# Which half of PSUM comes first: turning the pairs round behind two rounds, and when slots and squares are handed out

## The chip, the cores and the metric

The kernel runs on one core of one Trainium2 chip. The metric is the device time in microseconds of one execution; the median of three runs is taken. The profile and the trace are of one further execution on the same core.

## What is computed

The input `x` is a batch of 8 elements of 8 channels of 512 x 512 numbers in float32. Two layers follow each other.

Layer 0 normalizes each element by groups of channels, keeps a few low Fourier modes of every second row and column, mixes the channels in them with complex weights, transforms back and adds the result to `x`. Layer 1 normalizes again and computes three things from the result:

```python
for _ in range(STEPS):                      # 15 steps
    mapped = R * grid * (1.0 - grid)
    local = _conv(mapped, K_local, groups=C_OUT)          # 3x3, each channel by itself
    physics = (1.0 - EPS) * mapped + EPS * local
    grid = (1.0 - BETA) * physics + BETA * drive
cml_out = jnp.clip(grid, 0.0001, 1.0 - 0.0001)
h = jax.nn.relu(_conv(x, Wp, bp))                         # 3x3, 8 to 128 channels
nca_out = jax.nn.sigmoid(_conv(h, Wu, bu))                # 1x1, 128 to 8
gin = jnp.concatenate([x, cml_out, nca_out], axis=1)
g = jax.nn.sigmoid(_conv(jax.nn.relu(_conv(gin, Wg1, bg1)), Wg2, bg2))
return g * cml_out + (1.0 - g) * nca_out
```

## The kernel before

The program is written out without loops on the chip. Each engine gets its instructions in the order in which the Python source issues them, and waits by semaphores where data or a buffer is not ready. The source issues the work in ticks. An element takes 75 ticks (`TICKS`), called t = 0 to 74 here. One call of `work` is one tick, and in it stand, in this order:

- **Two sets of the 15-step loop.** A half element is 4 channels, cut into 5 sets. A set is a tile `m` of 128 partitions by 4 x 514: 4 slabs (or channels) of 32 rows, with 3 rows of overlap. It holds a squared form of the grid, so one step is a 3x3 convolution by 48 matmuls on 32 x 32 parts of the array (L536, 96 instructions in the profile), an addition of the drive by VectorE in two halves (L591), and a square by ScalarE (L597). The first set writes the pairs `pairs[:2]` of PSUM, the second `pairs[2:]`. PSUM is held as 4 pairs of two banks, so that is all of it.
- **None to two rounds** of the convolution from 8 to 128 channels (`Hidden.round`, L636), the first in `pairs[:2]`, the second in `pairs[2:]`. The relu of the first pair of each is ScalarE's (L642), that of the second pair VectorE's (L644). Both write one tile `h`.
- **Squares** (`Half.squares`, `Half.square`): before step 1 of a set, ScalarE makes its `m` from the drive `dE` (L516), and GpSimd fills the two border columns (L515). This is done in the tick before the set's first step.
- **Other work**, in this order: `others.first` (a gate convolution L706, or one or two pieces of the next element's layer 0, such as L338, L433, L401, L305, L313), then, after every second round, `hidden.point` (L655: 8 matmuls on the two `h` tiles of the last two rounds, the first round's four first; the result is copied into or added to `y`, L662 or L664, and after four rounds the sigmoid L668 follows), then `others.second` (a gate's point L723, or another piece of layer 0).
- **tick()**, which runs what was put off: `later(1, work)` runs work at the end of the next tick. The stores of finished sets (L577, in `leave`), of `y` (L671) and of layer 0's result, and the exchange of overlap rows (L566) come this way.

Of the four pairs, `work` gives the letters `a` (first piece or gate convolution), `b` (a second piece in front of the point), `c` (the point) and `d` (the gate's point, or a piece behind the point):

```python
a, b, c, d = (pairs[i] for i in ((0, 1, 3, 2), (2, 0, 3, 2))[rounds == 1])
```

SBUF tiles of the 15-step loop live in 15 slots (`Slots`), taken from the left of a queue of free names and put back at its right. Per half, 10 drives (`dE` and `dO` for each of 5 sets, four DMAs of 256 KB each, L494) and 5 tiles `m` need one. `Half.fetch` loads drives in each tick as long as slots are free; all of these DMAs, like nearly all others, are issued on SP's queue, in order. A drive is dropped in `settle` at one of the last two steps, an `m` in `store`, right behind the issue of its four stores. Squares of the first half fall in t = 74, 0 and 1, those of the second half in t = 36, 37 and 38.

After the last element's sets, 40 ticks of two rounds and six of none finish the rounds and gates that are left.

Of the kernel before, what the change touches and what calls it, by code (L numbers as in the profile page):

```python
# [128 lines left out]
def conv_layers(ctx: ExitStack, tc: tile.TileContext, a, out):  # L129
# [27 lines left out]
    sets, shared = Slots("set", 15), Slots("shared", SHARED)  # L157
# [7 lines left out]
    pairs = [pp.tile([P, 2, N], F32, name=f"pair{i}") for i in range(4)]  # L165
# [4 lines left out]
    def later(ticks, work):  # L170
        put_off.append((now[0] + ticks, work))

    def tick(end=False):
        now[0] += 1
        due = [w for at, w in put_off if end or at <= now[0]]
        put_off[:] = [] if end else [(at, w) for at, w in put_off if at > now[0]]
        for work in due:
            work()
# [296 lines left out]
    class Half:  # L475
# [27 lines left out]

        def squares(self, n):
            for k in range(SETS):
                if k - 2 in (n, n + 1):
                    self.square(k)

        def fetch(self, n):
# [21 lines left out]
    def convolve(m, c0, step, ps):  # L531
        for n, dx in enumerate((1, 0, 2)):
            for t in range(4):
                for h in range(4):
                    at = slice(32 * h, 32 * h + 32)
                    nc.tensor.matmul(  # L536
                        ps[h // 2][32 * t : 32 * t + 32, h % 2],
                        band[at, c0 + (t if step % 2 else h), dx],
                        m[at, t, dx : dx + N],
                        start=(n == 0), stop=(n == 2), tile_position=(32 * h, 32 * t),  # L540
                    )
# [26 lines left out]
    def leave(m, k, half):  # L568

        g = m[:, :, 1 : N + 1]  # L570
        nc.vector.tensor_scalar(g, g, 0.0001, 1.0 - 0.0001, ALU.max, ALU.min)  # L571

        def store():
            for h in range(4):
                s = 4 * k + h
                lo, hi = SHARES[s]
                nc.sync.dma_start(  # L577
                    out=half.cml[1 + STARTS[s] + lo : 1 + STARTS[s] + hi, half.c0 : half.c0 + 4],
                    in_=g[32 * h + lo : 32 * h + hi],
                )  # L580
            sets.drop(m)

        later(1, store)

    def settle(half, step, k, ps):

        m, d = half.m[k], half.d[k, step % 2]
        u = m[:, :, 1 : N + 1]
        for q in range(2):
            at = slice(2 * q, 2 * q + 2)  # L590
            nc.vector.scalar_tensor_tensor(  # L591
                u[:, at], ps[q], FLOOR, d[:, at], ALU.max, ALU.add
            )
            if q:
                yield
            if step < STEPS:
                nc.scalar.square(u[:, at], u[:, at])  # L597
        if step == 1:
            half.drive(k, 0)
        elif step == STEPS - 2:  # L600
            nc.gpsimd.tensor_scalar(d, d, 0.5, None, ALU.add)  # L601
        elif step >= STEPS - 1:
            sets.drop(d)
        if step == STEPS:
            leave(m, k, half)
        elif (step - k) % HALO == 0:
            later(1, lambda: renew(half.m, k, step))
# [284 lines left out]
    def work(sets, rounds, e, after, transfers, squares=lambda: None):  # L892

        settled = iter(())
        for (half, step, k), ps in zip(sets, (pairs[:2], pairs[2:])):
            convolve(half.m[k], half.c0, step - 1, ps)
            next(settled, None)
            settled = settle(half, step, k, ps)
            next(settled)
            others.finish()  # L900
        others.finish()
        transfers()
        for ps in (pairs[:2], pairs[2:])[:rounds]:
            e.hidden.round(ps, after, settled)
        next(settled, None)
        squares()

        a, b, c, d = (pairs[i] for i in ((0, 1, 3, 2), (2, 0, 3, 2))[rounds == 1])

        point = rounds and e.hidden.n % 2 == 0  # L910
        others.first([a, b if point else c])
        if point:
            e.hidden.point(c[:, 0])
        others.second([d if point else c])
        tick()

    elements = [e]
    for n in range(-FIRST_ROUNDS, 0, 2):
# [2 lines left out]
    for b in range(B):  # L921
# [5 lines left out]
        done, rounds = e.hidden.n, ROUNDS if after else ROUNDS_LAST  # L927
        for t in range(TICKS):
            assert not after or t < TICKS - 5 or not after.pieces
            halves = [(e.first, 2 * t), (e.second, 2 * t - TICKS)]  # L930
            if after:
                halves.append((after.first, 2 * t - 2 * TICKS))
            for half, n in halves:
                half.prepare(n)

            def squares():
                for half, n in halves:
                    half.squares(n)

            def transfers():  # L940
                others.feed(t)
                for half, n in halves:
                    half.fetch(n)

            now_sets = []
            for n in (2 * t, 2 * t + 1):
                half = (e.first, e.second)[n // TICKS]
                now_sets.append((half, n % TICKS // SETS + 1, n % SETS))

            more = done + (t + 1) * (rounds - done) // TICKS - e.hidden.n  # L950
            work(now_sets, min(more, 2 - e.hidden.n % 2), e, after and after.hidden, transfers, squares)
# [66 lines left out]
```

## Time and profile before

| what | value |
|---|---|
| median of three runs (lowest to highest) | 9907.52 us (9905.83 to 9934.52) |
| the profiled execution | 9903.73 us, its span 9901.9 us |
| TensorE busy | 9355.4 us, 94% |
| VectorE, ScalarE, GpSimd busy | 5876.2 (59%), 4301.9 (43%), 1762.5 us (18%) |
| granted TensorE clock, mean over the span | 0.988 |
| convolution of a set, L536 | 4093.8 us busy in 115200 instructions |
| rounds, L636 | 2862.1 us in 24576 |
| point, L655 | 995.0 us in 8192, 136.2 us idle before |
| squares, L516 | 80 of 1.99 us each |
| relus, L642 and L644 | 1024 each, 1.12 and 1.28 us each |
| moved in HBM | 992.42 MB read, 268.78 MB written, mean 127 GB/s |

A group's row gives the line of the source, the engine, the operation, output and inputs, the shapes and the count; behind the bar come the busy time and the mean of one in ns, then the engine's idle time just before these instructions and what ended most of it. In a row of waits stand who waited, for whom, and the total, the number and the longest. In the timeline stand the start and the duration in us, and in brackets the idle time before.

### The profile page before, as it was taken

Reading aid. Unit: us, or ns where it says so; the run is one execution under the profiler, and the core shown is the slowest. Engines: PE = TensorE matmul, PEld = TensorE weight load, DVE = VectorE, ACT = ScalarE, POOL = GpSimd, SP = SyncE. Lnnn points to the kernel's source line nnn. Section 1 sums busy time; section 2 is a strip of 40 time slices with the busy share of each in tenths; the row PEclk is TensorE's granted clock in tenths of the full one; section 3 lists DMA queues with packets and bytes.
Section 4 is the critical chain, followed back from the end, with each engine's and each line's share of the span. In section 5 each row is a group of like instructions: output and inputs, shape, how many; then the busy total and the mean of one; then the engine's idle time right before and its main releaser. Section 6 shows DMA issues by size and latency. Waiting matters only on the chain. (4 is left out here: it accounts for less than half of the span.)

```text
span 9901.9 us, 353033 instructions
## 1 busy us (share of the span) xinstructions
PE 9355.4 (94%) x160496; PEld 4299.0 (43%) x160496; DVE 5876.2 (59%) x6067; ACT 4301.9 (43%) x4445; POOL 1762.5 (18%) x1406
## 2 busy tenths in 40 slices
PE   6999999999999999999999999999999999898999
PEld 3444444444444434444344444444434444444433
DVE  5665555665566655666556655566555665555655
ACT  2544444443444434444444444445444454344423
POOL 2010111103121131111312013120221202221212
PEclk9999999999999999999999999999999999999999
DMA  5241355446544465445655356652665525753688
GB/s 152 86 121 34 80 141 135 138 126 167 139 129 142 129 162 138 133 128 136 163 140 143 117 141 162 145 157 94 148 164 139 161 97 142 171 124 95 147 200 202
DMA packets 625130, 1353.61 MB, mean 137 GB/s; under 512 B 72570, under 2 KB 72698, under 8 KB 593618
## 3 DMA queue, kind: packets, MB, share of 16 engines
q1 hardware_dynamic: 621280, 1329.89, 51.3%
q8 instruction: 1261, 20.66, 0.9%
q14 instruction: 235, 1.93, 0.1%
q10 hardware_dynamic: 2354, 1.14, 0.0%
HBM read 992.42 MB, written 268.78 MB: 127 GB/s over the span
## 5 line engine op out<-in xcount | busy, mean ns | idle before, releaser
L536 PE MATMUL pair<-m,band 32*32 32x512 f32 x115200 | 4093.8, 605 | 212.5 <-issue 99.6
L597 ACT ACTIVATE m<-m 128x1024 f32<-128x1024 f32 x2240 | 2363.7, 1055 | 2812.8 <-DVE m L591 2685.0
L536 PEld LDWEIGHTS pair<-m,band 32*32 32x32 f32 x115200 | 2258.3, 103 | 1955.8 <-issue 983.1
L636 PE MATMUL pair<-cols,w_p 32*128 32x511 f32 (+1 forms) x24576 | 2862.1, 603 | 47.0 <-issue 15.9
L591 DVE SCALAR_TENSOR_TENSOR m<-pair,dO 128x1024 f32<-128x1024 f32 x1280 | 1506.5, 1219 | 1384.6 <-PE pair L536 1214.6
L636 PEld LDWEIGHTS pair<-cols,w_p 32*128 32x128 f32 x24576 | 1275.9, 186 | 1645.0 <-issue 1116.1
L591 DVE SCALAR_TENSOR_TENSOR m<-pair,dE 128x1024 f32<-128x1024 f32 x1120 | 1318.8, 1219 | 1075.4 <-PE pair L536 870.9
L644 DVE TENSOR_SCALAR h<-pair,b_p 128x1024 f32<-128x1024 f32 x1024 | 1313.0, 1283 | 812.1 <-PE pair L636 803.3
L642 ACT ACTIVATE h<-pair,b_p 128x1024 f32<-128x1024 f32 x1024 | 1141.4, 1115 | 1044.1 <-PE pair L636 1043.9
L655 PE MATMUL pair<-h,w_u 128*32 128x512 f32 x8192 | 995.0, 598 | 136.2 <-DVE h L644 124.7
L729 POOL TENSOR_TENSOR mix<-mix 96x512 f32<-96x512 f32 x344 | 438.0, 1273 | 3809.0 <-ACT mix L727 3598.7
L706 PE MATMUL pair<-gin,w_g 128*32 128x511 f32 (+1 forms) x8256 | 965.9, 601 | 31.1 <-DMA gin<-nca 17.0
L711 POOL TENSOR_TENSOR mix<-mix 96x512 f32<-96x512 f32 x344 | 446.9, 1299 | 2006.1 <-DMA mix<-nca 1276.1
L601 POOL TENSOR_SCALAR dO<-dO 128x2048 f32<-128x2048 f32 x80 | 431.9, 5411 | 1228.5 <-DVE m L591 1228.5
L655 PEld LDWEIGHTS pair<-h,w_u 128*32 128x32 f32 x8192 | 249.0, 110 | 756.7 <-issue 384.7
L706 PEld LDWEIGHTS pair<-gin,w_g 128*32 128x32 f32 x8256 | 235.8, 110 | 711.3 <-issue 471.6
L668 ACT ACTIVATE y<-y,b_u 128x512 f32<-128x512 f32 x256 | 184.7, 721 | 808.5 <-DVE y L664 808.3
L734 DVE SCALAR_TENSOR_TENSOR mix<-mix,back 96x512 f32<-96x512 f32 x344 | 327.0, 951 | 147.3 <-POOL mix L729 147.3
L662 ACT COPY y<-pair 128x512 f32<-128x512 f32 x256 | 149.8, 585 | 599.8 <-PE pair L655 490.3
L716 DVE TENSOR_SCALAR mix<-pair,b_g 128x512 f32<-128x512 f32 x344 | 257.9, 750 | 247.8 <-PE pair L706 247.8
L723 PE MATMUL pair<-mix,w_g 128*32 128x512 f32 x2064 | 356.5, 593 | 10.5 <-DVE mix L716 8.5
L529 POOL TENSOR_SCALAR dO<-dO,base 128x512 f32<-128x512 f32 x320 | 238.6, 763 | 437.1 <-DMA dO<-xn 246.3
(86 smaller groups left out, 2661.4 us busy)
## 6 DMA issues: line engine op xcount, KB each, us to landing
gin<-xn SPq DMA_DIRECT2D x344, 384.0 KB
cols<-xn SPq DMA_DIRECT2D x256, 512.0 KB
x<-in_x SPq DMA_DIRECT2D x120, 1024.0 KB
gin<-cml SPq DMA_DIRECT2D x344, 320.0 KB
gin<-nca SPq DMA_DIRECT2D x344, 320.0 KB
dE<-xn SPq DMA_DIRECT2D x320, 256.0 KB
dO<-xn SPq DMA_DIRECT2D x320, 256.0 KB
mix<-xn SPq DMA_DIRECT2D x344, 192.0 KB
```

The lines of the kernel that those rows point to most:

```text
L536: nc.tensor.matmul(ps[h // 2][32 * t : 32 * t + 32, h % 2], band[at, c0 + (t if step % 2 else h), dx], m[at, t, dx : dx + N], start=(n == ...
L591: nc.vector.scalar_tensor_tensor(u[:, at], ps[q], FLOOR, d[:, at], ALU.max, ALU.add)
L597: nc.scalar.square(u[:, at], u[:, at])
L601: nc.gpsimd.tensor_scalar(d, d, 0.5, None, ALU.add)
L636: nc.tensor.matmul(ps[g // 2][:, g % 2, lo:hi], w_p[p, dx, i % 2], self.cols[p, i // 2, at : at + hi - lo], start=(n == 0), stop=(n == 2), ...
L642: nc.scalar.activation(h[:, :2], ps[0], AF.Relu, bias=b_p)
L644: nc.vector.tensor_scalar(h[:, 2:], ps[1], b_p, 0.0, ALU.add, ALU.max)
L655: nc.tensor.matmul(ps[32 * g : 32 * g + 32], w_u[:, r % 4], h[:, g], start=(r == self.hs[0][0]), stop=(r == self.hs[-1][0]), tile_position ...
L706: nc.tensor.matmul(ps[32 * j : 32 * j + 32, lo:hi], gband[:, dx], gin[:, j, at : at + hi - lo], start=(n == 0), stop=(n == 2), tile_positi ...
L711: nc.gpsimd.tensor_tensor(d, d, ng, ALU.subtract)
L723: nc.tensor.matmul(ps[at], gpoint[:, at], mix[:, 3], start=True, stop=True, tile_position=(0, 32 * j),)
L729: nc.gpsimd.tensor_tensor(d, d, mix[: GR * C, 2], ALU.mult)
```

## The change

Three things are changed.

1. Behind two rounds the letters are given anew: `a` and `d` are the first round's first pair, the point `c` is the first round's second pair, `b` is the second round's first pair. And the list of pairs is reversed, so the next tick begins in the half that the second round used. Behind one round the same pairs as before are used, behind none too.
2. The slot of a stored set is given back one tick after its stores are issued, not with them.
3. A square is made in its old place only if a slot is free there; otherwise a second call, behind `tick()`, makes it.

```diff
         def squares(self, n):
             for k in range(SETS):
-                if k - 2 in (n, n + 1):
+                if k - 2 in (n, n + 1) and k not in self.m and sets.free:
                     self.square(k)
...
-            sets.drop(m)
+            later(1, lambda: sets.drop(m))
 
         later(1, store)
...
-        for (half, step, k), ps in zip(sets, (pairs[:2], pairs[2:])):
+        near, far = pairs[:2], pairs[2:]
+        for (half, step, k), ps in zip(sets, (near, far)):
...
-        for ps in (pairs[:2], pairs[2:])[:rounds]:
+        for ps in (near, far)[:rounds]:
             e.hidden.round(ps, after, settled)
         next(settled, None)
         squares()
 
-        a, b, c, d = (pairs[i] for i in ((0, 1, 3, 2), (2, 0, 3, 2))[rounds == 1])
+        if rounds == 2:
+            (a, c), (b, _), d = near, far, near[0]
+            pairs.reverse()
+        elif rounds:
+            (a, c), (b, _), d = far, near, far[0]
+        else:
+            (a, b), (d, c) = near, far
...
         others.second([d if point else c])
         tick()
+        squares()
```

The order of TensorE's, VectorE's and GpSimd's instructions stays the same. Of the 80 squares, 30 move behind the tick. On SP's queue the drives' loads move: where 16 of them stood in one tick, eight come a tick later, behind the stores.

## The prediction

> **What bounds the kernel now.** I read the page's busy table and its row of granted clock, then the groups (who waits in front of TensorE), then the waits by name, and last the timeline of single ticks.
>
> ```profile
> PE 9355.4 (94%) x160496; PEld 4299.0 (43%) x160496; DVE 5876.2 (59%) x6067; ACT 4301.9 (43%) x4445; POOL 1762.5 (18%) x1406
> L536 PE MATMUL pair<-m,band 32*32 32x512 f32 x115200 | 4093.8, 605 | 212.5 <-issue 99.6
> L655 PE MATMUL pair<-h,w_u 128*32 128x512 f32 x8192 | 995.0, 598 | 136.2 <-DVE h L644 124.7
> PE pair L536 <- ACT m L516: 69.7, 21, 11.8
> POOL m L515 <- DMA cml<-m: 197.7, 28, 17.9
> ```
>
> TensorE works 94% of the span and takes its instructions in one order; the other engines have room. So the time is TensorE's work, which the change leaves as it is, plus its idle time: 9901.9 - 9355.4 = 546 us. Only idle time can be won. Two pieces of it lie where the change works: 136 us in front of the point matmuls (L655), and 70 us in which convolutions (L536) wait for squares (L516), whose memset in turn waits for a store to land.
>
> A tick of two rounds with nothing between rounds and point:
>
> ```profile
> 858.22 5.43 PE L636 MATMUL pair<-cols,w_p 32*128 32x512 f32 x48
> 863.74 1.28 DVE L644 TENSOR_SCALAR h<-pair,b_p 128x1024 f32<-128x1024 f32 x1 [1.29 <-PE pair L636]
> 863.74 1.11 ACT L642 ACTIVATE h<-pair,b_p 128x1024 f32<-128x1024 f32 x1 [0.51 <-PE pair L636]
> 865.17 1.92 PE L655 MATMUL pair<-h,w_u 128*32 128x512 f32 x16 [1.52 <-DVE h L644]
> 867.03 3.41 PE L536 MATMUL pair<-m,band 32*32 32x512 f32 x98
> ```
>
> The rounds end at 863.65. The first half of the point needs only the first round's `h`, long ready, but it writes `pairs[3]`, which the second round's relu (L644) is still reading: so all 16 wait 1.52 us. A tick of one round, where the pair is free, shows the same point without that:
>
> ```profile
> 8968.92 1.07 PE L655 MATMUL pair<-h,w_u 128*32 128x512 f32 x8
> 8969.03 1.11 ACT L642 ACTIVATE h<-pair,b_p 128x1024 f32<-128x1024 f32 x1 [0.43 <-PE pair L636]
> 8969.09 1.28 DVE L644 TENSOR_SCALAR h<-pair,b_p 128x1024 f32<-128x1024 f32 x1 [0.45 <-PE pair L636]
> 8970.19 0.38 PEld L655 LDWEIGHTS pair<-h,w_u 128*32 128x32 f32 x8 [1.11 <-ACT h L642]
> 8970.20 1.28 PE L655 MATMUL pair<-h,w_u 128*32 128x512 f32 x8 [0.21 <-ACT h L642]
> ```
>
> Eight run at once beside the relus, eight after them. From the end of the rounds to the end of the point it is 2.5 us (to about 8971.4), against 863.65 to 867.03 = 3.4 above: 0.9 us less.
>
> **The change part by part: the halves of PSUM.** No instruction of TensorE is added or moved; only the pairs differ. I call the pairs by their use in the tick: A, B (first round), C, D (second round). Behind two rounds the point goes from D to B, the gate's point from C to A, a second spectral piece from B to C, and the next tick starts on D, C. Ticks of one or no round keep their pairs. Of the 573 ticks with sets and rounds, 363 have two rounds. I sorted the timeline's two-round ticks by what stands between rounds and point:
>
> - Nothing: 46 ticks, and 4 before the first set. In 34 of them 0.9 us is won: 31. In 10 (t = 74 of seven elements, two in the first, one at the start) the first convolution then meets the square that is ready about 3.2 us behind the rounds (relu to 1.2, square 2.0); 0.1 each: 1. In 6 an L401 follows that waits for VectorE's chain (L393) anyway: 0.
> - L338 (eight short matmuls): 41 ticks with 0.37 us idle in front of L655, all of it won: 15.
> - L433: 41 ticks, 0.59 us each, all won: 24; less 1 where a square of 3.2 us is met (six at t = 38).
> - L305: 8 ticks, 1.12 us, of which 0.85 won: 7.
> - A gate convolution: 186 ticks, no idle before L655 now, nothing won. The gate's point now writes A, which L716 must have left. At 3575 L716 runs 3575.53 to 3576.28 and the gate's point starts at 3576.93: 0.6 us to spare. Cost 0; if L716 came more than 0.6 us later, it would cost the excess 180 times.
>
> Sum won: 77 us. Against it, a new wait. In two kinds of tick a second spectral piece (L401) stands in front of the point, and its pair is now C, held by ScalarE's relu of the second round, where B was long free:
>
> ```profile
> 2043.17 0.38 PE L313 MATMUL pair<-var,avg 128*128 128x1 f32 x2
> 2043.33 1.11 ACT L642 ACTIVATE h<-pair,b_p 128x1024 f32<-128x1024 f32 x1 [0.51 <-PE pair L636]
> 2043.48 1.06 PE L401 MATMUL pair<-e,om 16*32 16x512 f32 x8
> 2044.67 1.92 PE L655 MATMUL pair<-h,w_u 128*32 128x512 f32 x16
> ```
>
> L401 will wait to 2043.33 + 1.11 + 0.05 = 2044.5 instead of starting at 2043.48: 1.03 us, and behind it in TensorE's order the point and the next tick. 19 such ticks: 20 us. Where L433 is in front (14 ticks outside t = 37) L401 is 0.42 us late: 6. Net of this part: 77 - 26 = 51 us.
>
> **Slots and squares.** Now a square takes a slot dropped in the same tick() that issued its store, so memset, square and everything behind it on ScalarE stand until the store has landed:
>
> ```profile
> 1853.07 0.11 POOL L515 MEMSET m<- 128x8 f32 x1 [17.44 <-DMA cml<-m]
> 1853.21 2.00 ACT L516 ACTIVATE m<-dE,mhalf 128x2048 f32<-128x2048 f32 x1 [3.39 <-POOL m L515]
> 1855.27 1.92 PE L536 MATMUL pair<-m,band 32*32 32x512 f32 x4 [2.90 <-ACT m L516]
> 1858.26 8.05 PE L536 MATMUL pair<-m,band 32*32 32x512 f32 x188 [1.08 <-ACT ty L405]
> 8983.24 9.01 PE L536 MATMUL pair<-m,band 32*32 32x512 f32 x192 [11.76 <-ACT m L516]
> ```
>
> This is the tick behind t = 37. The first square now takes a slot that a drive set left in the same tick (no store on it), the second is issued behind the tick and takes one stored a tick earlier. SP's queue has at t = 36 eight loads of dE and dO instead of sixteen (about 1 us each), the other eight come at t = 37; what waits behind them, stores and `cols`, is 8 us earlier once and not later after. ScalarE's order becomes relu, square, L405, L668, square, so L405, which frees C for the next convolution, waits for one square (2 us), not two. Worked out on the tick at 5484 (rounds end 5484.2, relu to 5485.55): L401 5485.6 to 5486.6, point to 5488.45, convolution 1 to 5491.3, the late square (y added 5489.1, L668 5489.85) to 5491.85, convolution 2 to 5495.6; now the next rounds start at 5496.33. Won: 0.7. In three elements 0.7 each, and the same end applied to the other ticks: 3 (at 3060), 6 (at 1855), 4 (at 7901), 12.6 (at 8983, where 1.6 of 11.76 us remain). Sum 28 us. The squares' 4.03 us at t = 1 of every element stay: a first square behind L642 and L597, in the same order as now. All 30 squares that move behind the tick are for the second convolution, 2.8 us later than the first; 0.65 us at t = 37 is counted, the rest end in time.
>
> Two rules of the Trainium skill are weighed here. At 1858.26 the 188 matmuls took 8.05 us, at 5489.86 they took 6.54: 1.5 us more behind waits of 2.90 and 1.08 us. "TensorE: Matmul & The Clock Gate", Part 1 on the HAM gate, lets the clock fall to half only after an idle window of about 3.4 us; by that such waits cost themselves alone and the sum of 28 would be about 24 (three ticks, 1.5 each). I take the rows. And at 3589.22 L536 stands 4.85 us "<-issue" at a DMA share of 0.99: I read it as instructions not yet there. "Runtime: NRT & Kernel Launch", Instruction fetch mechanics, has the refill mostly hidden; by it, moving loads on the queues is worth nothing. By the trace 99.6 us of such idle stand before L536, most at t = 34 to 37 and 71 to 74, where the loads move. I take 0 for the middle and 25 us either way for the range.
>
> **Sum.** 51 + 28 = 79 us. The profiled execution took 9903.73 us (span 9901.9 and 1.8 around it), 3.8 under the median of 9907.52; 9903.7 - 79 = 9824.7, and at the median 9828.
>
> **The rivals.**
> - Nothing comes of it: what TensorE no longer waits for before the point, it waits for at the next convolution. For it: at t = 74 exactly that is foreseen. Against: in the timeline the next convolution follows the point at once, and in the new order its pairs D and C are free before the point's second half starts. It gives 9907, within 0.3%.
> - Less traffic at t = 36 also ends half of the "issue" idle, and the penalty behind it: 79 + 50, about 9778. Against: the bytes are the same.
> - Slower: the 30 late squares. Each is behind y (L662 or L668) and behind a memset on a slot stored one tick ago; if that store lands late, convolution 2 stands as convolution 1 did at 8983. From 79 / 30 = 2.6 us each it eats the gain; at 4 us with 1.5 us of half clock, 30 x 5.5 - 79 = 86 slower: 9994. Against: SP has one tick more, and now those memsets wait with no loss of TensorE.
>
> **How the numbers follow.** About 0.3% (30 us) is what a measurement of this kernel can tell from no change. The forecast (35 to 110 us won) 0.77; nothing comes of it 0.09; much more 0.09; slower 0.05. The range 9775 to 9872 leaves out no change and slower, and the far end of more. Faster 0.86, same 0.09, slower 0.05.
>
> **What would show it.** L655's idle of 136 us falls below 45, and its releaser is L642 or L644 inside the point. L401 shows a new idle of some 26 us on ACT h L642. The wait of L515 on the cml stores falls well under 198 us and the 11.76 us at 8983 is gone. PE's busy time stays at 9355. Wrong would be: L536's idle growing by what L655 lost, L723 waiting for L716, or convolution 2 waiting for L516.

## The result: 0.23% faster, some 23 us where 79 were forecast

Eight runs of each kernel: 9888.01 us after (9855.35 to 9908.01) against 9912.35 before (9905.83 to 9934.52). The ratio is 0.9977, its 95% interval 0.9967 to 0.9988: 23 us of 9912 are won, 12 to 33 by the interval. The direction was right; the time lies above the range (9775 to 9872). The profiled execution after took 9908.01 us, the slowest of its eight, so its span is read for where time went, not for the gain.

The page after, its row of busy engines and two groups:

```profile
PE 9436.7 (95%) x160496; PEld 4321.5 (44%) x160496; DVE 5882.7 (59%) x6067; ACT 4300.8 (43%) x4445; POOL 1771.2 (18%) x1406
L536 PE MATMUL pair<-m,band 32*32 32x512 f32 x115200 | 4119.5, 607 | 222.7 <-issue 123.6
L655 PE MATMUL pair<-h,w_u 128*32 128x512 f32 x8192 | 1038.5, 609 | 18.0 <-ACT h L642 16.6
```

And its waits by name (total, times, longest):

```profile
PE pair L401 <- ACT h L642: 27.3, 42, 0.9
PE pair L536 <- ACT m L516: 61.5, 31, 5.6
POOL m L515 <- DMA cml<-m: 82.6, 16, 9.3
```

The waits did what was forecast. L655's idle fell from 136 to 18 us, the memsets' wait for stores from 198 to 83, and L401 shows its new wait. All idle of TensorE, span less busy time, fell from 546.5 to 9906.2 - 9436.7 = 469.5: by 77 us. But the busy time of the same 160496 matmuls grew by 81.3 us, from 9355.4 to 9436.7. The waits were won and the matmuls became slower. Two single executions are compared here. The one before is 2 us faster than the fastest of its eight, and the one after has a clock of 0.982 where its eight runs have 0.982 to 0.985; so a middle run has somewhat less than 81 us of this.

The granted clock tells why. Core views, before and then after:

```profile
core 0: 9901.9 us, clock 0.988
```

```profile
core 0: 9906.2 us, clock 0.982
```

The trace's clock records hold 55 stretches at half speed before, 239.6 us together, and 76 after, 363.1 us. If a stretch at half clock loses half of its length, the 123.5 us more are 62 of the 81 us of busy time. The rest is not placed.

The stretches can be seen next to the new wait. The timeline after, at the tick that the prediction showed at 2043 before (start and duration, idle before in brackets):

```profile
2026.14 0.38 PE L313 MATMUL pair<-var,avg 128*128 128x1 f32 x2
2026.30 1.11 ACT L642 ACTIVATE h<-pair,b_p 128x1024 f32<-128x1024 f32 x1 [0.51 <-PE pair L636]
2027.47 1.06 PE L401 MATMUL pair<-e,om 16*32 16x512 f32 x8 [0.95 <-ACT h L642]
2028.46 3.18 PE L655 MATMUL pair<-h,w_u 128*32 128x512 f32 x16
2031.57 1.53 PE L433 MATMUL pair<-e,ty 8*128 8x512 f32 x4
```

L401 waits 0.95 us; 1.03 was forecast. But the 16 matmuls of L655 then take 3.18 us, not the 1.92 that they took in that tick before. The view by stretches of 1 us (length; busy time and instructions of TensorE, its weight loads, VectorE, ScalarE, GpSimd; then granted clock, DMA share, GB/s) shows the same tick after:

```profile
2026.00:2027.00 1.00, 0.52 (x6) 0.30 (x2) 0.70 (x1) 0.70 (x1) 0.00 (x0) 1.00 0.00 0
2027.00:2028.00 1.00, 0.53 (x8) 0.15 (x8) 0.59 (x1) 0.98 (x2) 0.00 (x0) 1.00 0.00 0
2028.00:2029.00 1.00, 1.00 (x16) 0.24 (x12) 0.00 (x0) 0.99 (x3) 0.00 (x0) 0.99 0.00 0
2029.00:2030.00 1.00, 1.00 (x12) 0.28 (x8) 0.98 (x4) 0.47 (x1) 0.00 (x0) 0.50 0.00 0
2030.00:2031.00 1.00, 1.00 (x8) 0.00 (x0) 1.00 (x2) 0.00 (x0) 0.00 (x0) 0.50 0.09 16
2031.00:2032.00 1.00, 1.00 (x6) 0.43 (x4) 0.83 (x1) 0.27 (x1) 0.00 (x0) 0.50 0.16 59
2032.00:2033.00 1.00, 1.00 (x4) 0.12 (x2) 0.00 (x0) 0.32 (x1) 0.00 (x0) 0.80 1.03 389
```

and before:

```profile
2043.00:2044.00 1.00, 1.00 (x14) 0.45 (x10) 0.67 (x1) 0.67 (x1) 0.00 (x0) 1.00 0.06 16
2044.00:2045.00 1.00, 0.87 (x12) 0.16 (x8) 0.61 (x1) 0.98 (x2) 0.00 (x0) 1.00 0.00 0
2045.00:2046.00 1.00, 1.00 (x15) 0.26 (x8) 0.00 (x0) 0.99 (x3) 0.00 (x0) 1.00 0.00 0
```

After, two microseconds pass with TensorE busy for half of each, and a microsecond later the clock is halved for some 3.4 us. Before, TensorE is busy for 1.00 and 0.87 of them and the clock stays at 1.00. L433 before:

```profile
2046.52 1.25 PE L433 MATMUL pair<-e,ty 8*128 8x512 f32 x4
```

The wait costs 1 us by itself and about 1.5 us more by the clock behind it (L655 3.18 - 1.92 = 1.26, L433 1.53 - 1.25 = 0.28).

### The profile page after: what moved, and what is told of

It is laid out like the page before. It is cut to its first block, busy times and chain, and to the rows that moved or that the text cites. A ratio compares the mean times of both kernels' runs of the same rounds, so it can differ in the third digit from the quotient of the medians.

```text
span 9906.2 us, 353389 instructions
## 1 busy us (share of the span) xinstructions
PE 9436.7 (95%) x160496; PEld 4321.5 (44%) x160496; DVE 5882.7 (59%) x6067; ACT 4300.8 (43%) x4445; POOL 1771.2 (18%) x1406
## 3 DMA queue, kind: packets, MB, share of 16 engines
q8 instruction: 1261, 20.66, 0.9%
## 5 line engine op out<-in xcount | busy, mean ns | idle before, releaser
L536 PE MATMUL pair<-m,band 32*32 32x512 f32 x115200 | 4119.5, 607 | 222.7 <-issue 123.6
L536 PEld LDWEIGHTS pair<-m,band 32*32 32x32 f32 x115200 | 2265.0, 104 | 1993.2 <-issue 1116.1
L636 PE MATMUL pair<-cols,w_p 32*128 32x511 f32 (+1 forms) x24576 | 2878.3, 605 | 45.0 <-DMA cols<-xn 14.1
L636 PEld LDWEIGHTS pair<-cols,w_p 32*128 32x128 f32 x24576 | 1288.9, 187 | 1651.1 <-issue 1144.9
L655 PE MATMUL pair<-h,w_u 128*32 128x512 f32 x8192 | 1038.5, 609 | 18.0 <-ACT h L642 16.6
L655 PEld LDWEIGHTS pair<-h,w_u 128*32 128x32 f32 x8192 | 252.8, 110 | 652.3 <-issue 355.1
L716 DVE TENSOR_SCALAR mix<-pair,b_g 128x512 f32<-128x512 f32 x344 | 258.1, 750 | 252.7 <-PE pair L706 252.7
L723 PE MATMUL pair<-mix,w_g 128*32 128x512 f32 x2064 | 359.1, 594 | 13.7 <-DVE mix L716 12.1
```

The lines of the kernel that those rows point to most:

```text
L536: nc.tensor.matmul(ps[h // 2][32 * t : 32 * t + 32, h % 2], band[at, c0 + (t if step % 2 else h), dx], m[at, t, dx : dx + N], start=(n == ...
L636: nc.tensor.matmul(ps[g // 2][:, g % 2, lo:hi], w_p[p, dx, i % 2], self.cols[p, i // 2, at : at + hi - lo], start=(n == 0), stop=(n == 2), ...
L655: nc.tensor.matmul(ps[32 * g : 32 * g + 32], w_u[:, r % 4], h[:, g], start=(r == self.hs[0][0]), stop=(r == self.hs[-1][0]), tile_position ...
L723: nc.tensor.matmul(ps[at], gpoint[:, at], mix[:, 3], start=True, stop=True, tile_position=(0, 32 * j),)
```

## The experiments

Two theories stood at first. A: the slots and squares bring their 28 us, and the pairs bring little, since L401's new wait is followed by half clock. B: L401's wait costs itself alone, the pairs bring their 51, and the slots and squares give it back. Ratios are against the kernel before on the same chip (median 9903.59 for each part alone, the old pairs' first run and the longer filler; 9914.89 on a second chip for the rest).

**One part alone.** The pairs, with slots and squares as before:

```diff
-                if k - 2 in (n, n + 1) and k not in self.m and sets.free:
+                if k - 2 in (n, n + 1):
...
-            later(1, lambda: sets.drop(m))
+            sets.drop(m)
...
-        squares()
```

> The pairs turned round as in the change, slots and squares as before. Theory A (the new wait of L401 costs its 26 us and in addition about 46 us of half clock behind it, because TensorE does almost nothing for two microseconds there): 77 won, 26 + 46 lost, so 5 us under before, no more than 0.15%. Theory B (L401's wait costs its 26 us alone, and what else was lost comes from the moved loads and late squares): 51 us under before, 0.5%, and a half-clock time close to the 240 us of before. Under A the half-clock time is about 330 us.

9897.77 us, ratio 0.9991 (0.9984 to 0.9998): 9 us won, near A. L655's idle is gone, yet the clock is 0.983. And the squares are waited for more than before (70 us there):

```profile
PE pair L536 <- ACT m L516: 99.2, 36, 14.5
```

Slots and squares, with the old pairs:

```diff
-        near, far = pairs[:2], pairs[2:]
-        for (half, step, k), ps in zip(sets, (near, far)):
+        for (half, step, k), ps in zip(sets, (pairs[:2], pairs[2:])):
...
-        for ps in (near, far)[:rounds]:
+        for ps in (pairs[:2], pairs[2:])[:rounds]:
...
-        if rounds == 2:
...
+        a, b, c, d = (pairs[i] for i in ((0, 1, 3, 2), (2, 0, 3, 2))[rounds == 1])
```

> Slots given back a tick later and the squares' second call, with the pairs as before. Theory A: this part does what was forecast, 28 us under before (0.28%), the 11.76 us wait for a square gone. Theory B: the moved loads bring stalls in the convolutions that the trace calls issue, and half clock behind them, 20 us and more; then this kernel is not faster than before, or slower.

9899.62 us, ratio 0.9991 (0.9985 to 0.9998): 9 us won, between the theories. The mechanism is there: the waits for squares fall, and the eight ticks behind t = 37, where it was to work, last 139.9 us in all against 168.1 before. That is the 28 us of the forecast. But the ticks at t = 0 last 137.3 us against 121.5, and more idle inside the convolutions has no releaser (99.6 us before):

```profile
PE pair L536 <- issue: 119.5, 69, 4.1
PE pair L536 <- ACT m L516: 55.6, 22, 5.5
```

So both theories were half right: each part gives back most of what it wins. The two parts add up: 9 + 9 = 18 against 23 measured for both, within the intervals.

**The wait taken out of the change.** Where two pieces stand in front of the point in a tick of two rounds, the letters are those of before and the list is not reversed; all else is as after (`used` is the number of pieces that `others.first` has issued):

```diff
...
         if rounds == 2:
-            (a, c), (b, _), d = near, far, near[0]
-            pairs.reverse()
+            a, b = near
...
         others.first([a, b if point else c])
+        if rounds == 2:
+            if others.used == 2:
+                d, c = far
+            else:
+                d, c = near
+                pairs.reverse()
```

> The changed kernel, except that in the two-round ticks with two spectral pieces in front of the point the old pairs are used (L401 in B, point in D, no reversal); all else as in the change. Theory A: L401's 26 us wait goes, and the half clock behind it with some 46 us: 72 us under the changed kernel, about 9816, ratio to before 0.990. Theory B: only the 26 us go, about 9862, ratio 0.995. In the trace A wants the half-clock time down from 363 to about 270 us.

9816.25 us (9802.87 to 9820.88), ratio 0.9907 (0.9894 to 0.992): A's number. With 41 waits of at most 0.95 us gone (one of the change's 42 stands in the kernel before and here too), some 69 us more are won than by the change, two and a half times what the waits last. The same tick here:

```profile
2012.18 0.38 PE L313 MATMUL pair<-var,avg 128*128 128x1 f32 x2
2012.49 1.06 PE L401 MATMUL pair<-e,om 16*32 16x512 f32 x8
2013.68 1.92 PE L655 MATMUL pair<-h,w_u 128*32 128x512 f32 x16
```

The same kernel on the other chip:

> The kernel with the old pairs in the ticks of L401 once more, beside the one with late slots for first halves only, so that the two stand against the same runs of before: ratio 0.9907 as measured, half-clock time about 260 us.

9812.67 us, ratio 0.9896 (0.9881 to 0.9911). By this ratio it is 80 us more than the change won.

**The wait put into the kernel before**, by one number:

```diff
-        a, b, c, d = (pairs[i] for i in ((0, 1, 3, 2), (2, 0, 3, 2))[rounds == 1])
+        a, b, c, d = (pairs[i] for i in ((0, 2, 3, 2), (2, 0, 3, 2))[rounds == 1])
```

> The kernel before with one letter changed: behind two rounds the second spectral piece goes to C instead of B, so L401 waits for ScalarE's relu in 41 ticks; nothing else differs. Theory A (wait and half clock behind it): 26 us for the wait and about 40 for the clock, 66 us slower than before, ratio 1.0065, half-clock time up from 240 to 320 us or more. Theory B (the wait alone): some 20 us slower (part of it lies where the point waits now anyway), ratio 1.002, half-clock time as before.

9966.82 us (9948.59 to 9977.83), ratio 1.0048 (1.0035 to 1.0061): 48 us slower by the ratio, nearer to A than to B. Its new wait and its busy engines:

```profile
PE pair L401 <- ACT h L642: 27.3, 42, 0.9
PE 9386.0 (94%) x160496; PEld 4305.7 (43%) x160496; DVE 5875.1 (59%) x6067; ACT 4302.2 (43%) x4445; POOL 1762.2 (18%) x1406
```

The waits of L401 hold 27 us. All idle of TensorE is 18 us more than before (span 9950.7 less 9386.0, against 546.5), and the same matmuls are busy 31 us longer (9386.0 - 9355.4): together 49, the measured 48. Not every wait did it: 25 half-clock stretches fell into the 41 ticks, and at 1997 and 2053 L655 took its 1.92 us behind a wait of 0.95:

```profile
1997.75 1.06 PE L401 MATMUL pair<-e,om 16*32 16x512 f32 x8 [0.95 <-ACT h L642]
1998.74 1.92 PE L655 MATMUL pair<-h,w_u 128*32 128x512 f32 x16
```

Which waits do it can be read from the clock records. In all ten traces every stretch at half clock begins on a fixed grid of 3.413 us, to within 1 ns. In a tick with a wait of 0.95 us, 2.25 us pass from the end of the rounds to the first matmul of the point, and in them TensorE waits or runs matmuls that use little of it (128 x 1, or 16 rows). The three kernels with the bare wait (the change, the pairs alone and this one) have 60 such ticks. In 38 of them the rounds end between 0.06 us before and 1.28 us after a point of the grid, so that all or nearly all of the 2.25 us lies between two such points; in each of these L655 took 2.4 us or more. In the other 22 the rounds end 1.38 to 3.27 us after a point, and in each of these L655 took its 1.92 us. So it is the place of the stretch on the grid that decides between ticks that look alike, and that shifts with all that ran before. Without the wait the stretch is 1.4 to 1.8 us, and L655 took its 1.92 us in all 41 ticks of the kernel before.

**The wait filled with work.** Is it the idle time that lowers the clock, or the place of L401's output? In the change as it is, extra matmuls whose result nobody reads were put in front of L401, into the other bank of the point's pair. First one or two of 512 columns in each of these ticks:

```diff
...
+            if fill and bank[-1] is fill[0]:
+                for _ in range(more):
+                    nc.tensor.matmul(fill[1][:, 1], avg, fill[2][:, 0], start=True, stop=True)
...
-                ty_next = over_rows(c + 1)
+                ty_next = over_rows(c + 1, 1 if c % 2 or not c else 2)
```

> The changed kernel with its wait of L401 left as it is, but one or two additional 128 x 128 matmuls of 512 columns, whose result nobody reads, put in front of L401 where it waits (0.4 to 0.9 us of work in 41 ticks, into the unused second bank of the point's pair). Theory A: TensorE stays busy, the half clock behind L401 does not come, and the kernel with more work is about 40 us faster than the changed one: 9845, ratio 0.993. Theory B: the wait is what costs; no difference to the changed kernel (0.9977), or slower by the work added.

9879.27 us, ratio 0.9974 (0.9967 to 0.9982): no better than the change, and no answer, since the filler was too long:

```profile
L402 PE MATMUL pair<-cols,avg 128*128 128x512 f32 x120 | 62.1, 625 | 0.0
```

It lasts 62.1 us where 27 us were to be filled. (The half clock in these ticks was gone with it, as the table below shows.) So it was cut to fit: 512 columns where the wait was 0.95 us, 192 where it was 0.42.

```diff
...
+            if fill and bank[-1] is fill[0]:
+                nc.tensor.matmul(
+                    fill[1][:, 1, :more], avg, fill[2][:, 0, :more], start=True, stop=True
+                )
...
-                ty_next = over_rows(c + 1)
+                ty_next = over_rows(c + 1, 192 if c % 2 or not c else N)
```

> As the filled kernel, but the additional matmul is cut to the wait: one of 512 columns (1.04 us) where the wait is 0.95, one of 192 columns (about 0.4 us) where it is 0.42. The 60 matmuls of the first filling took 62 us of TensorE for 26 us of waits, so about 33 us were added to the path; cut to fit, none are. Theory A: about 40 us under the changed kernel, ratio to before 0.993 to 0.994. Theory B: as the changed kernel, 0.9977.

9833.56 us (9828.21 to 9840.94), ratio 0.9916 (0.9903 to 0.993): better than A's .993. The program does 34 us more work on the engine that bounds it, and is some 60 us faster than the change:

```profile
L401 PE MATMUL pair<-cols,avg 128*128 128x192 f32 (+1 forms) x82 | 34.0, 497 | 0.0
PE 9409.2 (96%) x160578; PEld 4320.6 (44%) x160578; DVE 5882.5 (60%) x6067; ACT 4301.6 (44%) x4445; POOL 1772.0 (18%) x1406
```

Busy time is 27.5 us lower than in the change (9436.7), with the filler in it. The same tick (the lines of the file are 1 to 5 later here; L406 is the former L401, L660 the former L655):

```profile
2021.77 0.38 PE L314 MATMUL pair<-var,avg 128*128 128x1 f32 x2
2022.02 1.10 PE L401 MATMUL pair<-cols,avg 128*128 128x512 f32 x2
2023.10 1.06 PE L406 MATMUL pair<-e,om 16*32 16x512 f32 x8
2024.09 1.92 PE L660 MATMUL pair<-h,w_u 128*32 128x512 f32 x16
```

L401's piece still starts late, at the relu's end, in the same pair as in the change; only TensorE is busy meanwhile. So it is the idle time and not the place. The 21 us by which the kernel without the wait is faster still, on the same chip, are about what the waits themselves last: of the 80 us some 60 are the clock's. In the 41 ticks of this kind, by the trace:

| kernel | ticks, sum us | stretches at half clock that begin in them, us | in the whole span, us |
|---|---|---|---|
| before | 686.1 | 27.3 | 239.6 |
| the change | 740.8 | 119.5 | 363.1 |
| pairs alone | 742.9 | 88.7 | 340.7 |
| wait in the kernel before | 744.2 | 109.2 | 328.9 |
| slots alone | 669.3 | 10.2 | 250.5 |
| old pairs there | 674.2 | 10.2 | 258.2 |
| filled | 726.2 | 10.2 | 284.7 |
| filled to fit | 701.5 | 10.2 | 254.3 |

In all three kernels with the bare wait these ticks are 55 to 58 us longer than before. (The eight of them behind t = 37 gain in the change by the slots, which hides part of its cost.)

**The slots at t = 0.** What is left is the 28 us of the slots, of which alone 9 remained. If the loads that come a tick later are what makes t = 0 longer, the slot should be given back late only where that is useful, for sets of the first half, on top of the old pairs there:

```diff
-            later(1, lambda: sets.drop(m))
+            if half.c0:
+                sets.drop(m)
+            else:
+                later(1, lambda: sets.drop(m))
```

> The kernel with the old pairs in the ticks of L401, and slots given back a tick later for the first halves only (sets that end at t = 35 to 37); those of the second halves (t = 72 to 74) at once as before. Theory C: the late slot pays at t = 37 (28 us) and costs at t = 0 (about 14 us, loads and instruction fetch meeting there); then this kernel is 10 to 15 us under the one with all slots late, about 9803. Rival: the idle called issue at t = 0 differs by chance; then no difference, within 5 us.

9799.11 us (9791.4 to 9809.46), ratio 0.9882 (0.9868 to 0.9895). It is the fastest of all, 14 us under the run with late slots everywhere on the same chip, whose lowest, 9810.48, is above its highest. The eight ticks at t = 0 last 118.3 us against 136.7, those behind t = 37 144.2 against 149.5. TensorE at one t = 0 in the timeline, with late slots everywhere:

```profile
4811.39 5.47 PE L536 MATMUL pair<-m,band 32*32 32x512 f32 x155 [0.61 <-ACT m L516]
4820.78 2.74 PE L536 MATMUL pair<-m,band 32*32 32x512 f32 x37 [3.92 <-issue]
4823.45 5.50 PE L636 MATMUL pair<-cols,w_p 32*128 32x512 f32 x24
```

and with them in first halves only (L639 is the former L636):

```profile
4814.59 5.47 PE L536 MATMUL pair<-m,band 32*32 32x512 f32 x155 [0.61 <-ACT m L516]
4820.37 2.12 PE L536 MATMUL pair<-m,band 32*32 32x512 f32 x37 [0.31 <-issue]
4822.42 2.85 PE L639 MATMUL pair<-cols,w_p 32*128 32x512 f32 x24
```

The stop inside the convolution falls from 3.92 to 0.31 us, and the 24 matmuls behind it no longer take 5.50 us instead of 2.85. The two ticks by stretches, in the same order:

```profile
4811.00:4833.00 22.00, 13.65 (x219) 5.33 (x219) 6.60 (x6) 10.14 (x10) 9.74 (x13) 0.83 0.90 228
```

```profile
4815.00:4830.00 15.00, 10.66 (x232) 4.74 (x216) 5.99 (x5) 9.92 (x9) 7.33 (x10) 0.93 0.50 168
```

A DMA share of 0.90 and a clock of 0.83 stand against 0.50 and 0.93: with the late slots the loads run during this tick. The last issue of loads in or before it, with late slots everywhere and then in first halves only:

```profile
4811.21 3.77 SPq L494 DMA_DIRECT2D dO<-xn  x4
```

```profile
4806.95 1.76 SPq L494 DMA_DIRECT2D dO<-xn  x4
```

This tick and one other make up 13 of the 18 us (6.9 and 6.3); the other six, from 2.2 us longer to 4.4 us shorter, make the rest. Over the whole span this idle is no smaller (111.1 us against 98.1), so what is shown is that it left t = 0, not that there is less of it. Two executions of the same kernel, the old pairs there on the two chips, differ as much (117.0 and 98.1), so the 20 us more of the slots alone say little by themselves.

What TensorE lacks in these stops can be read from the trace. One queue carries instructions:

```profile
q8 instruction: 1261, 20.66, 0.9%
```

That is 16384 bytes a packet, and TensorE ran some 322,900 instructions, its waits for semaphores included, so a packet holds 256 of them. All 662 stops that the ten traces call issue before the convolution (L536), 73 of them in this kernel, stand at the same place, within one instruction, of a block of 256 in TensorE's order, and each ends 1.2 to 1.8 us after a packet of this queue landed. TensorE waited for its instructions.

## Why the prediction was wrong

**The step that failed** is the term for L401: "19 such ticks: 20 us", and 6 for the 0.42 us. The wait was 26 to 27 us, as worked out. What was left out is the clock behind it: in the kernel before with only this wait, 48 us in all, 31 of it longer matmuls; in the change more, where taking the wait out won 69 us on one chip and 80 on the other. The sum's own ground was "TensorE's work, which the change leaves as it is", and "PE's busy time stays at 9355" was one of the rows that were to show it right. It did not stay: 9436.7. The prediction had the right row in hand, the 8.05 us of L536 behind a stall, and took it over the page's window of about 3.4 us of idle. But it used it only for the stalls that go, not for the one that comes.

**Second, the slots and squares**: 28 us was right for the ticks behind t = 37 (28 measured in the part alone, 20 in the change). What the same delay does at t = 0 was taken as 0 in the middle; those ticks are 14 us longer in the change and 16 in the part alone. The 25 us set aside for the moved loads covered it in size, but the middle leaned to the wrong side. The rule that the refill is mostly hidden ("Runtime: NRT & Kernel Launch", Instruction fetch mechanics) was weighed for this: idle without a releaser, up to 3.92 us at once, stands where the loads stand. The prediction read it as instructions not yet there, and the blocks of 256 above bear that out. By count the page is right, since 59 of the 1261 packets before and 73 after have such a stop behind them; but these stops add up to 99.6 and 123.6 us.

**Right in size:** the 77 us of waits in front of the point. The median tick of each kind lost 0.95 us (0.9 forecast) with nothing between, 0.44 with L338 (0.37), 0.64 with L433 (0.59), 0.87 with L305 (0.85). L655's idle is 18, under 45. The gate's point waits 12.1 us for L716 against 8.5 before, so the slack of 0.6 us held. The 11.76 us at 8983 are 1.55:

```profile
8985.55 7.64 PE L536 MATMUL pair<-m,band 32*32 32x512 f32 x192 [1.55 <-ACT m L516]
```

**The rivals.** The 30 late squares did not come late: the second convolutions, which are the ones that need them, waited 1.4 us for squares in all, against 2.6 before. Less traffic did not help. "Nothing comes of it" was nearest to the time, by another mechanism than the one given: not the next convolution waited, the clock did.

With the two terms corrected the sum is near. 77 + 28 - 15 for t = 0 gives 90 without the wait, where 92 and 103 were measured on the two chips. For the wait and its clock there is one size from outside the change, the 48 us of the kernel before; with it 42 us would be left, and 23 were measured. The 69 and 80 us are differences of the measured gains themselves, so they can't test the sum. Why the wait costs more in the change than in the kernel before is not settled.

## What to carry to other kernels

On a TensorE that bounds the kernel, price a new wait by the clock records behind it and not by its length: a wait of 1 us beside matmuls that use little of TensorE cost about two to three times itself (48 to 80 us for 26), and taking its 41 cases out of the change raised its gain from 0.2% to 0.9% or 1.0%. Read busy time as well as idle time when a change is said to move waits only, since the same matmuls grew by 81 us between the two profiles. And when a resource is given back later, look at every place where it is used: late slots paid in one half of each element and cost 14 us in the other.

## What was not expected of the hardware

- The clock halves without a long idle window. "TensorE: Matmul & The Clock Gate", Part 1, speaks of an idle window of about 3.4 us; here 0.95 us of waiting, between matmuls of 128 x 1 and of 16 rows, in 2 us with TensorE half busy, left 27 stretches at half clock in 41 ticks, where 7 were before. The length of the half-clock stretch, about 3.4 us, is the page's own figure. A wait of 1.52 us between the rounds and the point did not do it in the kernel before: in the tick at 858 that the prediction showed, L655 took its 1.92 us. What decides between ticks that look alike is where they fall on the grid of 3.413 us: 38 of 60 were slowed and 22 were not, without an exception. How little TensorE may do between two points of the grid before the clock halves is not measured here.
- Unread matmuls of 34 us made the kernel about 60 us faster, and brought the half clock from 363 to 254 us.
- TensorE stood for up to 5.5 us at once (with the wait put into the kernel before) because its instructions were not there, always at the same place of a block of 256.
